# A two-layer block in float32 on one core: the first loads on two queues, two weight products moved ahead of the first transposes, and no subtraction on GpSimd

## The chip, the cores and the metric

The kernel runs on one core of a Trainium2 chip. The metric is the device time of one execution in microseconds; the time of a kernel is the median of several runs. A core has five engines with an instruction queue each: TensorE (PE, matrix products; its weight loads are listed apart as PEld), VectorE (DVE), ScalarE (ACT), GpSimd (POOL) and SyncE (SP, here used only to issue DMA transfers). Each engine takes its instructions in the order that was fixed when the program was built.

## The reference

The input x has 4 sequences of 512 tokens of 256 features. Two layers follow, both of the form x + s * silu(f):

```
xn = layernorm(x)                                    # no scale, no shift
layer 0: s = xn + rmsnorm(((xn W_in^T) * g) W_out^T) * norm_w     # g: one number per channel, from B and C
layer 1: s = xn + causal_attention(layernorm(xn) * gamma + beta) o_proj
both:    f = fwht(silu(xn W1^T) * (xn W3^T)) W2^T    # hidden size 1024, fwht = Walsh-Hadamard transform
x = x + s * silu(f)
```

Everything is float32. The state of the layer 0 mixer is zero at its start and is not carried, so that the mixer is one matrix M = W_in^T diag(g) W_out^T. The transform is symmetric and is applied to W2 in place of the hidden values. In layer 1 the products q k^T and v o_proj need only Wq Wk^T / 16 and Wv o_proj, two products of weights.

## The kernel before, in words

A float32 operand is kept as a pair (hi, lo), hi rounded by ScalarE (a cast, L61) and lo = value - hi by a subtraction (L62), mostly on VectorE; `split` (L59) does both. A float32 product is three products of such parts (`mm3`, L64). Products of weights (`product_of_weights`, L153: wqk, wvo, m) take float32 operands directly.

The work runs sequence by sequence: for b in 0 to 3 the feed-forward block of layer 0 (`ffn`, L310), then the four of layer 1. A feed-forward block has 8 chunks of 128 hidden channels. A chunk c is two up products of 12 matmuls in all into two PSUM banks (f_0gu in the first block, of three banks in the tag), ScalarE's silu of the first bank (L363), VectorE's gate product with the second bank (L364, f_0h), the split of the result (into f_0hh and f_0hl, or into the spare tiles early in the first block), and 12 down products (f_0dn, L332). In the first block all down products come after all up products, since W2 is not ready earlier.

Other work is cut into steps and laid beside the chunks (`Beside`, L530): preparing W2 (`prep_w2`, L113: three butterfly stages of two VectorE operations for each half of the columns, tiles w2b, then a product with the Hadamard matrix into w2ps and a split into w2h and w2l), the mixer, the norm of the next sequence, attention. The build orders the instructions of each engine with a planner: it simulates the program with its own durations and takes, on each engine, the ready instruction that stands earliest in the program. `tc.issue_after(ins)` (L307, L330, L350, L373) pins the instructions of a block behind one instruction of the same engine.

The start (L573 to L629): SyncE issues the four tiles of x for b = 0, then ident, qk, the first part of w13, vo, the second part of w13, w2 (two halves), and the rest (L583 to L594). At the same time TensorE multiplies zeros seven times (L581). `norm_first` (L263) normalises the four token tiles one by one and transposes each (two 128x128 transposes into a PSUM bank, tile xt_0tp), and splits the result into xth and xtl. Then `w13(0)` splits the first part of w13 (`split_w13`, L97, in two halves), and `prep_first` (L607) forms wqk (L608), the three butterfly stages of the first half of w2 and wvo (L615), all ahead of the first block. The parts of w13 that are split later come from `ffn` itself (L351), where each is pinned behind the gate of two chunks before. For parts 2 and 3 the subtraction is on GpSimd (L102); the pin acts on the engines of the gate and so not on GpSimd. The PSUM tag "ms" has three banks, shared by the zero products, the products of weights and the transposes.

Of the kernel before, what the change touches and what calls it, by code (L numbers as in the profile page):

```python
# [12 lines left out]
# float32 kept to the 12 significant bits that one pass of the tensor engine multiplies  # L13
# exactly. A float32 value is the exact sum of two of these (hi + lo), so a float32 product
# is three passes: hi*hi + hi*lo + lo*hi; lo*lo lies below float32's rounding.
# [6 lines left out]
P = 128  # L22
# [6 lines left out]
DS = 16  # L29
# [6 lines left out]
def kernel(ctx: ExitStack, tc: tile.TileContext, a: dict, out: bass.AP):  # L36
# [22 lines left out]
    def split(src, hi, lo, engine=nc.vector):  # L59
        """hi + lo = src, exactly."""  # L60
        nc.scalar.copy(hi, src)  # L61
        engine.tensor_tensor(lo, src, hi.bitcast(F32), ALU.subtract)  # L62

    def mm3(o, terms):  # L64
        """o = sum over terms of lhs.T @ rhs, each operand a pair (hi, lo)."""
        seq = [(l[0], r[0]) for l, r in terms]
        for l, r in terms:
            seq += [(l[0], r[1]), (l[1], r[0])]
        for n, (l, r) in enumerate(seq):
            nc.tensor.matmul(o, l, r, start=n == 0, stop=n == len(seq) - 1)  # L70

# [20 lines left out]
    def load_w13(layer, q):  # L92
        raw = t4(f"w13raw_{layer}_{q}", [P, 2, S])
        nc.sync.dma_start(raw, a[f"w13_{layer}"][q])
        return raw

    def split_w13(layer, q, raw):  # L97
        hi = wp.tile([P, 2, S], F32R, tag="w13h", name=f"w13h_{layer}_{q}", bufs=4)
        lo = wp.tile([P, 2, S], F32R, tag="w13l", name=f"w13l_{layer}_{q}", bufs=4)
        for c in range(2) if (layer, q) == (0, 0) else (slice(None),):  # L100
            cs = slice(c * D, (c + 1) * D) if c in (0, 1) else c
            engine = nc.gpsimd if layer == 0 and q >= 2 else nc.vector  # L102
            split(raw[:, :, cs], hi[:, :, cs], lo[:, :, cs], engine)
        return hi, lo
# [8 lines left out]
    def prep_w2(layer, raws, dst, scratch):  # L113
        """Rows of W2 under the Walsh-Hadamard transform (it is symmetric, so it may act on
        W2 in place of the hidden values): over the 8 blocks by butterflies, over the 128
        rows of a block by a product with the +-1/32 matrix."""
        w2h, w2l = dst
        for half in range(2):
            ds_ = slice(half * P, (half + 1) * P)
            cur = raws[half]  # L120
            for st, h in enumerate((1, 2, 4)):
                nxt = scratch(f"w2b{st}_{layer}_{half}", [P, NH, P])
                cv = cur.rearrange("p (g two h) d -> p g two (h d)", two=2, h=h)
                nv = nxt.rearrange("p (g two h) d -> p g two (h d)", two=2, h=h)
                nc.vector.tensor_tensor(nv[:, :, 0], cv[:, :, 0], cv[:, :, 1], ALU.add)  # L125
                nc.vector.tensor_tensor(nv[:, :, 1], cv[:, :, 0], cv[:, :, 1], ALU.subtract)
                cur = nxt
                yield
            # in float32 it costs TensorE two passes more, but no split beforehand
            native = layer == 0 and half == 0  # L130
            if not native:
                bh = t4(f"w2bh_{layer}_{half}", [P, NH, P], F32R)
                bl = t4(f"w2bl_{layer}_{half}", [P, NH, P], F32R)
                split(cur, bh, bl)
                yield
            for q in range(2):
                o = psum(f"w2ps_{layer}_{half}_{q}", [P, NH // 2, P])
                qs = slice(q * NH // 2, (q + 1) * NH // 2)
                if native:
                    nc.tensor.matmul(o, had_f, cur[:, qs, :], start=True, stop=True)  # L140
                else:
                    nc.tensor.matmul(o, had, bh[:, qs, :], start=True, stop=False)
                    nc.tensor.matmul(o, had, bl[:, qs, :], start=False, stop=True)
                split(o, w2h[:, qs, ds_], w2l[:, qs, ds_])
                yield
# [6 lines left out]

    def product_of_weights(name, lhsT, rhs, nk, scale=None):  # L153
        """[256, 256] = lhsT.T @ rhs over nk chunks of 128, in float32, as a (hi, lo) pair."""
        hi = wp.tile([P, 2, D], F32R, name=f"{name}h")
        lo = wp.tile([P, 2, D], F32R, name=f"{name}l")
        o = psum(f"{name}ps", [P, 2, D])
        for i in range(2):
            for k in range(nk):
                nc.tensor.matmul(  # L160
                    o[:, i, :], lhsT(k, i), rhs(k), start=k == 0, stop=k == nk - 1
                )
        if scale is None:
            split(o, hi, lo)
        else:
            nc.scalar.mul(hi, o, scale)
            nc.vector.scalar_tensor_tensor(lo, o, scale, hi.bitcast(F32), ALU.mult, ALU.subtract)
        return hi, lo
# [9 lines left out]
    def prep_m(win, wout):  # L178
        """xi*(sum of C_real*B_real - C_imag*B_imag) between W_in and W_out is one matrix."""
# [16 lines left out]
    def load_pair(name):  # L196
        raw = t4(f"{name}raw", [P, 2, 2, D])
        nc.sync.dma_start(raw, a[name])
        return raw
# [12 lines left out]
    def moments(name, x, mr):  # L212
        """mr[:, 0] = the tokens' means, mr[:, 1] = their 1 / sqrt(variance + eps)"""
# [10 lines left out]
    def layernorm(name, x, y, groups=(NT,)):  # L224
        """y = layernorm(x), the token tiles in groups of these sizes"""
# [37 lines left out]
    def norm_first():  # L263
        """norm(0, 0), each token tile on its own"""
# [4 lines left out]
        layernorm("ln0_0", xs[0], xn, (1,) * NT)  # L269
        for t in range(NT):  # L270
            o = psum(f"xt0_0tp{t}", [P, 2, P])
            for k in range(2):
                nc.tensor.transpose(o[:, k, :], xn[:, t, sl(k)], ident)
            split(o, hi[:, :, sl(t)], lo[:, :, sl(t)])

    def norm(layer, b):
# [6 lines left out]
        if layer:  # L283
            # The second normalisation acts on the transposed values: its moments as rows of
            # all tokens, in every partition.
# [24 lines left out]
    def ffn(name, xT, w13, w2, slot, defer=1, spare=(), last=None, parts=1, behind=False):  # L310
        """Up, silu gate, down with the transformed W2: two PSUM banks of two token tiles.
        The down products of a chunk follow the up products of the defer-th after it.
        spare: pairs of tiles that hold the split hidden values of the first chunks.
        last: called with each token tile's result, finished one after the other, each in a
        bank of its own."""
# [8 lines left out]
        def down(c, hh, hl, tiles=range(NT)):  # L324
            for t in tiles:
                o = outs[t]
                for n, (l, r) in enumerate(((hh, w2h), (hh, w2l), (hl, w2h))):
# [8 lines left out]
                    # A start clears the accumulate bits of its whole bank: the bank's second  # L336
                    # tile begins without one, behind the first's.
# [44 lines left out]
        # the later tokens' products stay behind, for the ends of the earlier tokens to run beside  # L382
# [11 lines left out]
    def gate(name, dn, s, x, store=None):  # L394
        """x += s * silu(dn), a pair of token tiles at a time."""
# [9 lines left out]
    def mixer(b):  # L405
        """xn += rmsnorm(xn @ M) * norm_w"""
# [21 lines left out]
    def attention(b):  # L428
        """The transposed xn, split; then xn += causal attention of the normalised, scaled and
        shifted xn"""  # L430
# [30 lines left out]
        def scores(i0):  # L461
            """Masked scores of two query tiles"""
# [11 lines left out]
        def softmax(i0, scs):  # L474
            """The two exponentials follow each other, for ScalarE changes its table for them."""
# [54 lines left out]
    class Beside:  # L530
        """Steps of other work, spread over the slots of a feed-forward block."""
# [27 lines left out]
    def some(gen, n):  # L559
        """The next n steps of gen"""  # L560
# [8 lines left out]
    # steps of each; an attention's first ones (up to its scores) run a phase ahead of the rest  # L569
    NORM, MIXER, ATT, ATT1, W2P = 3, 3, 18, 6, 12  # L570

# [1 line left out]
    load_x(0, 1)  # L573
    # TensorE's clock rises only after a while of work: these products of zeros run while the
    # first loads are under way.
# [5 lines left out]
    for i in range(7):  # L581
        nc.tensor.matmul(warm, zr[:, :P], zr, start=True, stop=True)
    nc.sync.dma_start(ident, a["ident"])  # L583
    qk = load_pair("qk")
    raw13 = [load_w13(0, 0)]
    vo = load_pair("vo")
# [8 lines left out]
    norm_first()  # L595
# [7 lines left out]
    w13(0)  # L603
    w2 = w2_tiles(0)
    first = {}

    def prep_first():  # L607
        first["wqk"] = prep_qk(qk)  # L608
        nc.scalar.copy(had, had_f)
        yield  # L610
        steps = prep_w2(0, raw2, w2, x_slot)
        for _ in range(3):
            next(steps)
        yield
        first["wvo"] = prep_vo(vo)  # L615
# [7 lines left out]
    dn = None  # L623
    for b in range(B):
        tasks = []
        if b == 0:
            prep = prep_first()
            for _ in range(3):
                next(prep)  # L629
# [70 lines left out]
def _rows(w):  # L700
    """[r*128, n] -> [128, r, n]"""
# [3 lines left out]
def _w13(w1, w3):  # L705
    """Columns of W1.T and W3.T in turns of 128, in four parts of [128, 2, 512]."""
# [4 lines left out]
def _w2(w2):  # L711
    """W2.T as [half of d][128, 8 blocks, 128]."""
# [46 lines left out]
```

## Time and profile before

The median of 3 runs is 374.34 us (374.17 to 375.75).

| what | before |
|---|---|
| median of the runs | 374.34 us |
| profiled execution, first to last instruction (span) | 370.9 us |
| own time of the profiled execution beside that span | the page gives none; the median of the runs is 3.4 us above the span |
| TensorE busy | 361.5 us, 97% |
| VectorE busy | 248.0 us, 67% |
| ScalarE busy | 179.7 us, 48% |
| GpSimd busy | 36.2 us, 10% |
| DMA moved, 0 to 5 us and 5 to 12 us | 127 and 383 GB/s |
| first up product starts | 9.8 us |

The profile is one execution, recorded by the hardware. Its times start with the first instruction. A row names the line of the kernel, the engine and the tiles (out<-in); "[2.5 <- ...]" or a line of the waits says how long an engine stood idle and whose result ended that. The chain of work is followed back from the last instruction, at each step to what released it. Ends of matmuls are modelled, so a busy TensorE is not one at its peak. A duration of one operation is longer than the distance to the next on the same engine, since neighbours overlap at their ends.

### The profile page before, as it was taken

How to read it: one execution, taken by the hardware profiler on the slowest of the kernel's cores; microseconds unless marked ns; L12 is line 12 of the kernel's file. 1: busy time of each engine (PE TensorE's matmuls, PEld its weight loads, DVE VectorE, ACT ScalarE, POOL GpSimd, SP SyncE). 2: the span in 40 equal slices, each digit the busy share in tenths (PEclk: the TensorE clock that was granted, in tenths of full speed). 3: DMA queues.
4: the chain of work that ended last, by engine and by line, in shares of the span. 5: the costliest groups of instructions: out<-in, count | busy, mean ns of one | idle time of the engine just before them, and what ended most of it. 6: DMA issues, size and time to landing. Idle time of an engine off the chain costs nothing.

```text
span 370.9 us, 5491 instructions
## 1 busy us (share of the span) xinstructions
PE 361.5 (97%) x2167; PEld 318.2 (86%) x2167; DVE 248.0 (67%) x519; ACT 179.7 (48%) x334; POOL 36.2 (10%) x30
## 2 busy tenths in 40 slices
PE   6997999999999999999999999999999999999995
PEld 4875999888888898889888998988989898888895
DVE  6898948996499339945949487465846447374644
ACT  2765334624453335445553654266633646356451
POOL 2060023410025002400011000010000000000000
PEclk9999999999999999999999999999999999999999
DMA  7915200000000040110010001100003000010001
GB/s 234 389 51 203 80 2 1 2 0 2 0 3 0 0 171 0 58 57 2 1 59 0 0 2 57 59 1 2 0 2 114 2 0 1 2 57 2 1 2 57
DMA packets 8969, 15.50 MB, mean 42 GB/s; under 512 B 848, under 2 KB 6640, under 8 KB 8944
## 3 DMA queue, kind: packets, MB, share of 16 engines
q1 hardware_dynamic: 8944, 15.16, 11.7%
q8 instruction: 17, 0.28, 0.3%
q14 instruction: 8, 0.07, 0.1%
HBM read 13.04 MB, written 2.11 MB: 41 GB/s over the span
## 4 chain that ended last, share of the span: by engine, by line
PE 90%; DVE 5%; DMA 2%; SPq 1%; issue 0%; ACT 0%; DVEq 0%
PE f_3gu L70 12%; PE f_2gu L70 12%; PE f_1gu L70 12%; PE f_0gu L70 8%; PE f_0dn L332 6%; PE f_3dn L332 6%; PE f_1dn L332 6%; PE f_2dn L332 6%; PE sc L70 4%; PE pv L70 4%; PE o L70 3%; PE v L70 3%; PE tq L70 3%; DMA w2raw<-in_w 2%; DVE w2b L125 1%; PE pt L498 1%
## 5 line engine op out<-in xcount | busy, mean ns | idle before, releaser
L70 PE MATMUL f_0gu<-xtl,w13h 128*128 128x512 f32 (+1 forms) x68 | 25.8, 382 | 0.0
L70 PE MATMUL f_1gu<-xth,w13l 128*128 128x512 f32 x64 | 25.5, 399 | 0.0
L70 PE MATMUL f_0gu<-xth,w13l 128*128 128x512 f32 (+1 forms) x68 | 25.5, 384 | 0.0
L70 PE MATMUL f_3gu<-xtl,w13h 128*128 128x512 f32 x64 | 25.5, 398 | 0.0
L70 PE MATMUL f_2gu<-xth,w13l 128*128 128x512 f32 x64 | 25.3, 396 | 0.0
L70 PE MATMUL f_3gu<-xth,w13l 128*128 128x512 f32 x64 | 25.3, 396 | 0.0
L70 PE MATMUL f_1gu<-xtl,w13h 128*128 128x512 f32 x64 | 25.3, 396 | 0.0
L70 PE MATMUL f_2gu<-xtl,w13h 128*128 128x512 f32 x64 | 25.3, 395 | 0.0
L70 PE MATMUL f_0gu<-xth,w13h 128*128 128x512 f32 (+1 forms) x68 | 21.3, 393 | 2.5 <-DVE f_0h L364 2.5
L364 DVE TENSOR_TENSOR f_2h<-f_2h,f_2gu 128x512 f32<-128x512 f32 x16 | 10.9, 681 | 19.1 <-PE f_2gu L70 11.0
L61 ACT CAST f_2hh<-f_2h 128x512 fp32r<-128x512 f32 x16 | 9.9, 621 | 23.0 <-DVE f_2h L364 23.0
L70 PE MATMUL f_2gu<-xth,w13h 128*128 128x512 f32 x64 | 20.7, 397 | 0.0
L70 PE MATMUL f_1gu<-xth,w13h 128*128 128x512 f32 x64 | 20.7, 398 | 0.0
L70 PE MATMUL f_3gu<-xth,w13h 128*128 128x512 f32 x64 | 20.6, 397 | 0.0
L61 ACT CAST f_3hh<-f_3h 128x512 fp32r<-128x512 f32 x16 | 9.9, 620 | 19.7 <-DVE f_3h L364 19.7
L332 PE MATMUL f_3dn<-w2l,f_3hh 128*128 128x256 f32 x64 | 17.6, 281 | 0.0
L332 PE MATMUL f_2dn<-w2l,f_2hh 128*128 128x256 f32 x64 | 17.6, 282 | 0.0
L332 PE MATMUL f_3dn<-w2h,f_3hh 128*128 128x256 f32 x64 | 17.5, 281 | 0.0
L332 PE MATMUL f_2dn<-w2h,f_2hh 128*128 128x256 f32 x64 | 17.5, 281 | 0.0
L332 PE MATMUL f_1dn<-w2l,f_1hh 128*128 128x256 f32 x64 | 17.4, 281 | 0.0
L332 PE MATMUL f_1dn<-w2h,f_1hh 128*128 128x256 f32 x64 | 17.3, 281 | 0.0
L363 ACT ACTIVATE f_2h<-f_2gu 128x512 f32<-128x512 f32 x16 | 9.5, 596 | 16.0 <-PE f_2gu L70 16.0
(227 smaller groups left out, 1104.4 us busy)
## 6 DMA issues: line engine op xcount, KB each, us to landing
w13raw<-in_w SPq DMA_DIRECT2D x8, 512.0 KB, 6.2
w2raw<-in_w SPq DMA_DIRECT2D x4, 512.0 KB, 6.8
mrb<-there SPq DMA_DIRECT2D x4, 512.0 KB, 3.7
x<-in_x SPq DMA_DIRECT2D x3, 512.0 KB, 3.7
out<-x SPq DMA_DIRECT2D x6, 256.0 KB, 2.1
x<-in_x SPq DMA_DIRECT2D x4, 128.0 KB, 2.2
qkraw<-in_qk SPq DMA_DIRECT2D x1, 512.0 KB, 4.7
voraw<-in_vo SPq DMA_DIRECT2D x1, 512.0 KB
```

The costliest lines, as they stand in the source:

```text
L61: nc.scalar.copy(hi, src)
L70: nc.tensor.matmul(o, l, r, start=n == 0, stop=n == len(seq) - 1)
L125: nc.vector.tensor_tensor(nv[:, :, 0], cv[:, :, 0], cv[:, :, 1], ALU.add)
L332: return nc.tensor.matmul(o, l[:, sl(t)], r[:, c, :], start=start, stop=stop, skip_group_check=True)
L363: nc.scalar.activation(h, gu[0], AF.Silu)
L364: gates.append(nc.vector.tensor_tensor(h, h, gu[1], ALU.mult))
L498: nc.tensor.transpose(pt[:, sl(j)], p[:, sl(j)], ident)
```

## The change

ident, qk and vo are issued by ScalarE, directly behind the issue of x by SyncE; the first part of w13 follows on SyncE. The zero products are five instead of seven. The product wqk is formed ahead of the first transposes, which are pinned behind its last matmul; wvo is formed between the transposes of tiles 1 and 2, pinned in the same way. The split of the first w13 part is pinned behind the splits of tile 1, and the first butterflies of w2 behind the last low part of tile 3. The subtraction of every w13 part is on VectorE. `last_product` remembers the last matmul of each product of weights.

```diff
-    def load_w13(layer, q):
+    def load_w13(layer, q, queue=nc.sync):
         raw = t4(f"w13raw_{layer}_{q}", [P, 2, S])
-        nc.sync.dma_start(raw, a[f"w13_{layer}"][q])
+        queue.dma_start(raw, a[f"w13_{layer}"][q])
...
-            engine = nc.gpsimd if layer == 0 and q >= 2 else nc.vector
-            split(raw[:, :, cs], hi[:, :, cs], lo[:, :, cs], engine)
+            split(raw[:, :, cs], hi[:, :, cs], lo[:, :, cs])
...
+    last_product = {}
...
-                nc.tensor.matmul(
+                last_product[name] = nc.tensor.matmul(
...
     def load_pair(name):
         raw = t4(f"{name}raw", [P, 2, 2, D])
-        nc.sync.dma_start(raw, a[name])
+        nc.scalar.dma_start(raw, a[name])
...
+        behind, lo_ = last_product["wqk"], None
         for t in range(NT):
+            if t == 2:
+                with after(behind):
+                    first["wvo"] = prep_vo(vo)
+                behind = last_product["wvo"]
             o = psum(f"xt0_0tp{t}", [P, 2, P])
-            for k in range(2):
-                nc.tensor.transpose(o[:, k, :], xn[:, t, sl(k)], ident)
-            split(o, hi[:, :, sl(t)], lo[:, :, sl(t)])
+            with after(behind):
+                for k in range(2):
+                    behind = nc.tensor.transpose(o[:, k, :], xn[:, t, sl(k)], ident)
+            hi_ = nc.scalar.copy(hi[:, :, sl(t)], o)
+            lo_ = nc.vector.tensor_tensor(
+                lo[:, :, sl(t)], o, hi[:, :, sl(t)].bitcast(F32), ALU.subtract
+            )
+            if t == 1:
+                with after(hi_), after(lo_):
+                    w13(0)
+        return lo_
...
     load_x(0, 1)
+    nc.scalar.dma_start(ident, a["ident"])
+    qk = load_pair("qk")
+    vo = load_pair("vo")
+    raw13 = [load_w13(0, 0)]
...
-    for i in range(7):
+    for i in range(5):
         nc.tensor.matmul(warm, zr[:, :P], zr, start=True, stop=True)
-    nc.sync.dma_start(ident, a["ident"])
-    qk = load_pair("qk")
-    raw13 = [load_w13(0, 0)]
-    vo = load_pair("vo")
     raw13 += [load_w13(0, 1)]
...
-    norm_first()
+    first = {"wqk": prep_qk(qk)}
...
-    w13(0)
+    normed = norm_first()
     w2 = w2_tiles(0)
-    first = {}
 
     def prep_first():
-        first["wqk"] = prep_qk(qk)
         nc.scalar.copy(had, had_f)
-        yield
         steps = prep_w2(0, raw2, w2, x_slot)
-        for _ in range(3):
-            next(steps)
-        yield
-        first["wvo"] = prep_vo(vo)
+        with after(normed):
+            for _ in range(3):
+                next(steps)
         yield
...
             prep = prep_first()
-            for _ in range(3):
-                next(prep)
+            next(prep)
```

## The prediction

> **What bounds the kernel now.** I read four views: the busy times of the page, the waits of TensorE, the chain of work cut to the first 45 us, and the order of time of VectorE and GpSimd in the stretch where TensorE stands still. First the busy times (us, share of the span, instructions), then who TensorE waited for over the whole span (us in total, times, longest).
>
> ```profile
> PE 361.5 (97%) x2167; PEld 318.2 (86%) x2167; DVE 248.0 (67%) x519; ACT 179.7 (48%) x334; POOL 36.2 (10%) x30
> ```
>
> ```profile
> PE f_0gu L70 <- DVE f_0h L364: 2.5, 1, 2.5
> PE warm L582 <- DVE zr L579: 1.9, 1, 1.9
> PE xt_0tp L273 <- DVE ln_0r L237: 0.5, 1, 0.5
> PE xt_0tp L273 <- DVE xtl L62: 0.3, 1, 0.3
> PE xt_0tp L273 <- DVE xn L240: 0.2, 1, 0.2
> ```
>
> TensorE is the bound: from 31.4 us to its last product it waits for nothing. So an edit can gain only in what stands in front: one stall of 2.5 us, three small ones before the first transposes (1.0 us together), and a start at 5.8 us, ahead of which there are only products of zeros. Everything later can only get worse. The chain shows who sets the end of the 2.5 us stall (start, us, what):
>
> ```profile
> 4.96 7.99 DMA w2raw<-in_w
> 12.97 0.69 DVE w2b L125
> ...
> 15.59 0.60 DVE wvol L62
> 16.19 0.59 DVE f_0h L364
> 16.79 1.14 DVE w13l L62
> ...
> 22.13 2.24 DVE early L62
> 24.36 2.81 DVE w2b L125
> ...
> 30.17 0.60 DVE w2b L126
> 30.77 0.61 DVE f_0h L364
> 31.38 0.04 issue
> 31.43 1.66 PE f_0gu L70 x6
> ```
>
> From the landing of the first w2raw at 12.95 to 31.4 us VectorE works without a pause, and TensorE waits for the gate product (L364) at its end, which frees a PSUM bank of the up products. Two links of that chain are about four times too long. Beside them lies GpSimd (start, us, engine, line, shape, count):
>
> ```profile
> 20.31 6.31 POOL L62 TENSOR_TENSOR w13l<-w13raw,w13h 128x1024 fp32r<-128x1024 f32 x2 [13.46 <-ACT w13h L61]
> ...
> 22.04 2.32 DVE L62 TENSOR_TENSOR early<-f_0h,early 128x512 fp32r<-128x512 f32 x1
> 24.29 2.88 DVE L125 TENSOR_TENSOR w2b<-w2b 128x512 f32<-128x512 f32 x1
> 27.09 0.68 DVE L126 TENSOR_TENSOR w2b<-w2b 128x512 f32<-128x512 f32 x1
> ```
>
> The same two operations take 0.68 us each elsewhere (median of the w2b rows 0.68, of the early rows 0.68) and follow each other 0.60 apart. The two long ones both read two SBUF tiles while GpSimd reads two. They start at 22.04 and 24.29, the next at 27.09: (2.25 - 0.60) + (2.80 - 0.60) = 3.85 us lost.
>
> **The change, part by part.**
>
> No split on GpSimd: the two low-part subtractions of w13 parts 2 and 3 (3.50 and 2.87 us on GpSimd) become VectorE's. Price: the row of part 1, 128x1024 at 1.22 us, 1.14 to the next instruction; two of them 2.28 us. VectorE wins back the 3.85. Net -1.57 us of VectorE time.
>
> Both now carry a wait: the part 2 split stands behind chunk 2's gate on VectorE, part 3 behind chunk 4's. Behind them queue the butterflies, low parts and gates of the later chunks, and TensorE waits for those through its PSUM banks. Whether one or both fall ahead of chunk 3's gate (the one that ended the stall) isn't visible, so I keep +1.14 and +2.28.
>
> Product of vo ahead: its eight products take 1.73 us (0.216 apart) whichever place they have, so TensorE's work is unchanged; but wvol (0.60 us in the chain at 15.59) leaves the chain.
>
> Start of the chain: the w2 butterflies now wait for the last low part of the first transposes, tile 3. I put that at 11.6 us below, when w2raw has landed too (12.95 before; the loads come earlier, see below). Against 12.97: -1.3.
>
> The gate at the end of the chain, at 31.4, so moves by -3.85 - 0.60 - 1.3 + (1.14 to 2.28) = -4.6 to -3.5, to 26.8 to 27.9 us. TensorE arrives at 28.9 (28.4 with the start below). The 2.5 us stall goes with 0.5 to 1.6 us to spare. That margin is the cover of the added 2.28; gone, each further us on VectorE is a us of TensorE. Next late would be part 3's low part: chunk 4 ends on TensorE at about 26.9, gate and split follow by 28.6, chunk 6 wants it at about 30. ScalarE loses nothing: its casts for these parts stay.
>
> Two queues. SyncE issues one load per 0.47 us, so qk went out as the sixth. With the page's DMA rates by stage (us, PE, PEld, DVE, ACT, POOL busy, clock, DMA share, GB/s):
>
> ```profile
> 0.00:5.00 5.00, 3.09 (x7) 2.15 (x7) 2.81 (x10) 1.28 (x1) 0.58 (x6) 1.00 0.59 127
> 5.00:12.00 7.00, 5.96 (x32) 4.48 (x32) 5.21 (x17) 3.29 (x8) 1.84 (x4) 1.00 0.96 383
> ```
>
> The first 5 us move 127 GB/s, the next seven 383. ScalarE can issue ident, qk, vo from 0.73 (three issues at 0.43 beside its table load of 1.28 us, 2.6 us in all before its first cast, which came at 6.5). Here a rule speaks against the edit: the Trainium skill, "DMA: Bandwidth & Descriptors", section "Issuing engines are not separate DMA queues", says that all issuers share the same 16 engines and a second one saves only issue time. By it nothing is won once they are full; by the row they are not full for the first 5 us. qk was issued at 3.06 and landed 4.7 us later, 7.8. Issued at 1.2, with the x tiles beside it, x + ident + qk are 1.1 MB: at 383 GB/s from 2.4 us on, 5.3. Both ends: 4.3 (qk preferred) and 7.8 (no gain). I take 5.2. vo now precedes the first w13 part (2.2 MB in all): 2.4 + 2.2/0.383 = 8.1, against 9.1 before. If the second queue wins nothing it is 9.1 + 1.3 = 10.4. SyncE's own queue loses three issues, so w13 and w2raw go out 1.4 us sooner. The price falls on x: its four tiles landed by 4.6 and now share the engines, to 5.3 by the same sum, 7 if the big packets of qk and vo are preferred. Tile 0 needed 2.9 us from its landing to its normalised value, the later ones some 2, and their transposes stand behind the two products (7.4 and 10.2 below), which hides it.
>
> TensorE's start. Transposes are ordered behind the qk product, tiles 2 and 3 behind vo's. Five zero products instead of seven end near 4.1. A second rule is against it: "TensorE: Matmul & The Clock Gate", Part 1, grants the full clock only after some 3.4 us of sustained work. The row: the zero products' weight loads took 330 ns, those of the transposes 143 (median; up to 229, at 5.8 us), and no stage shows a granted clock other than 1.00, so the rise can be placed only at about 6.3. If it stays there, the qk product runs 5.2 to 7.4 (2.5 of its eight at half speed). If the gap before qk costs one more window, half of 3.4 us, 1.7, is lost: the end would be 371.3 + 1.7 = 373.0. I take the first, as the qk product itself fills the stretch.
>
> Then: transposes of two tiles 0.6 (8.0); vo's product needs one of three PSUM buffers, free when the qk result is copied (0.60 ScalarE, 0.68 VectorE): 0.5 of waiting (8.5); product 1.7 (10.2); two tiles 0.6 (10.8), low part of tile 3 by 11.6. The up products start at about 10.9, under w13's cast. Before, TensorE had both products and all transposes behind it at 12.93, with 13 half-width up products (0.117 apart, 1.5 us) mixed in: 11.4. Gain 0.5; with the ends of qk's landing -1.5 to +1.4.
>
> Sum: -2.5 (stall) - 0.5 (start) = -3.0 on a span of 370.9, 367.9. The profile gives no other time of its own; the runs' median is 374.34, 3.4 above the span. With that unchanged: **371.3 us**.
>
> **The rivals.** A measurement of this kernel can tell about 0.5% from no change: 372.5 to 376.2 is "the same".
>
> *The start eats the gain.* The stall goes, but the clock rises a window later (-1.7), or qk lands near 7.8, pinning the transposes behind it (up to 2.0 worse than my value). 371.3 + 1.7 = 373.0. For it: DMA share is 0.96 from 5 us on, and all loads share it; TensorE idles about 1 us before qk. Against: the first 5 us are half empty. The form in which the edit doesn't do what it says (the second queue moves nothing) is the milder end: gain 0 in place of 0.5, 371.8.
>
> *VectorE becomes the bound of the first block: slower.* In 11 to 41 us it is busy 27.3 of 30. If the order written out by the planner puts the part 2 split behind all butterflies (twelve at 0.60, the low parts and gates of three chunks), it comes at 11.6 + 7.2 + 1.2 + 1.1 + 1.8 + 1.8 + 1.1 = 25.8, where TensorE wants it at about 24: 1.8 of stall at chunk 4; with gate 4 late by as much, part 3 behind the mixer's and the next norm's work (4.2 us of statistics at 39.5) stalls chunk 6 by up to 4. Total 5.8 against 2.5 before, less 0.5: 377.1. It decides once the two splits come over 4.9 us late together. Against: without GpSimd VectorE has 1.57 us less to do.
>
> **How the numbers follow.** Stall gone: 0.60, own range 370.0 to 372.4 (qk landing early to the second queue useless, and a stall of half a us left). Gain eaten: 0.24, about 373, to 375. Slower: 0.16, about 377. So faster 0.60, same 0.24, slower 0.16. The range leaves out some 0.05 below 370.0 and most of the slower case above 376.3.
>
> **What would show it.** No GpSimd row at L62; early and w2b rows all near 0.68; no wait of TensorE for f_0h near 28; qk landing by 5.5 and the first 5 us above 200 GB/s; qk product from about 5.2, with weight loads falling from 330 to 190 ns within it; up products from about 11; nothing new after 41 us. I am wrong if TensorE waits for w13l in chunks 4 or 6, if the qk product starts near 7.8, or if weight loads stay at 330 ns past 7 us.

## The result, and the profile after

The changed kernel takes 374.38 us (median of 20 runs), the kernel before 373.91 (20 runs, taken beside it). The ratio is 1.001, with a 95% interval of 0.999 to 1.003: no difference that can be measured. The forecast was 371.3 us, faster. Seven of the 20 executions take 372.2 to 373.1 us at a mean granted clock of 0.997 to 1.000, thirteen take 374.1 to 376.6 us, ten of these at 0.989 to 0.995.

The profiled execution has a span of 370.4 us, against 370.9; it took 372.17 us, the least of the 20. Each execution takes 1.8 to 2.0 us more than its span, so of the 3.4 us that the forecast added to the span only about 1.8 lie outside it. The rest means that the profile of the kernel before, too, shows an execution shorter than the median (by estimate 370.9 + 1.8 = 372.7 us). First the waits of TensorE after the change (us in total, times, longest):

```profile
PE warm L602 <- DVE zr L599: 1.9, 1, 1.9
PE wvops L161 <- DVE wqkl L168: 1.5, 1, 1.5
PE wqkps L161 <- DMA qkraw<-in_qk: 0.8, 1, 0.8
PE f_0dn L347 <- ACT w2h L61: 0.4, 1, 0.4
```

The stall of 2.5 us on the gate product is gone. In its place stands a wait of the vo product for the low part of the qk product, 1.5 us, with two smaller ones (the 1.9 us are the start of the program, as before). The long VectorE rows are gone too (order of time, VectorE, the same stretch as before):

```profile
22.17 0.68 DVE L62 TENSOR_TENSOR early<-f_0h,early 128x512 fp32r<-128x512 f32 x1
22.77 0.68 DVE L379 TENSOR_TENSOR f_0h<-f_0h,f_0gu 128x512 f32<-128x512 f32 x1
23.37 1.22 DVE L62 TENSOR_TENSOR w13l<-w13raw,w13h 128x1024 fp32r<-128x1024 f32 x1
24.50 0.68 DVE L124 TENSOR_TENSOR w2b<-w2b 128x512 f32<-128x512 f32 x1
...
28.10 0.68 DVE L379 TENSOR_TENSOR f_0h<-f_0h,f_0gu 128x512 f32<-128x512 f32 x1
...
30.70 1.22 DVE L62 TENSOR_TENSOR w13l<-w13raw,w13h 128x1024 fp32r<-128x1024 f32 x1
```

Every early and w2b operation is at 0.68 us, the two added low parts (w13l) take 1.22 each as the forecast priced them, and TensorE waits for neither. What went wrong lies before all this. The chain of work of the changed kernel, cut to the start (start, us, what):

```profile
2.10 6.29 DMA x<-in_x
...
8.41 0.44 DVE ln_0st L234
...
9.33 0.56 POOL ln_0r L239
...
9.91 0.28 DVE xn L241
...
10.24 0.70 DVE wqkl L168
...
10.98 1.99 PE wvops L161 x8
12.97 0.48 PE f_0gu L70 x4
```

The last tile of x (tile 3, counted from 0) landed at 8.4 us; before the change it had landed by 4.6. VectorE does that tile's norm, which includes a step on GpSimd, and then the low part of the qk product (wqkl), whose inputs had been ready since 9.6. This low part is the last reader of the qk product's PSUM bank, and of the three shared banks it is the one that the vo product gets; so the vo product waits for it. The up products start at 12.6 us where the forecast had 10.9, and where the kernel before started at 9.8 with part of its products still to do. The DMA rates by stage, and the rows of the qk product:

```profile
0.00:5.00 5.00, 2.50 (x5) 1.49 (x5) 2.40 (x8) 1.28 (x1) 0.86 (x6) 1.00 0.64 201
5.00:12.00 7.00, 5.29 (x17) 4.12 (x18) 4.61 (x15) 3.01 (x6) 1.66 (x3) 1.00 0.99 387
```

```profile
L161 PEld LDWEIGHTS wqkps<-qkraw x8: 288/337/337, 5.2 to 7.9; 128*128 128x128 f32 x8
L161 PE MATMUL wqkps<-qkraw x8: 634/634/796, 5.2 to 8.3; 128*128 128x256 f32 x8
```

The second queue did fill the first 5 us (201 GB/s, before 127), and qk landed at 5.13. But the qk product ran at half speed to its end: its eight matmuls took 3.6 us (5.17 to 8.75), where the vo product's took 1.6 (10.98 to 12.62), and its weight loads 337 ns where the vo product's took 190. The clock column stands at 1.00 in both stages, so this slow start shows in the durations alone.

### The profile page after: what moved, and what is told of

Same layout as the page of the kernel before. It is cut to its first block, busy times and chain, and to the rows that moved or that the text cites. A ratio compares the mean times of both kernels' runs of the same rounds, so it can differ in the third digit from the quotient of the medians.

```text
span 370.4 us, 5483 instructions
## 1 busy us (share of the span) xinstructions
PE 361.8 (98%) x2165; PEld 318.9 (86%) x2165; DVE 244.8 (66%) x521; ACT 179.7 (49%) x334; POOL 33.1 (9%) x28
## 3 DMA queue, kind: packets, MB, share of 16 engines
q1 hardware_dynamic: 8512, 14.05, 10.9%
## 4 chain that ended last, share of the span: by engine, by line
PE 96%; DMA 2%; DVE 1%; SPq 0%; ACT 0%; issue 0%; POOL 0%
PE f_0gu L70 12%; PE f_3gu L70 12%; PE f_2gu L70 12%; PE f_1gu L70 12%; PE f_0dn L347 6%; PE f_3dn L347 6%; PE f_1dn L347 6%; PE f_2dn L347 6%; PE sc L70 4%; PE pv L70 4%; PE o L70 3%; PE v L70 3%; PE tq L70 3%; DMA x<-in_x 2%; PE pt L513 1%; PE mps L161 1%
## 5 line engine op out<-in xcount | busy, mean ns | idle before, releaser
L70 PE MATMUL f_0gu<-xth,w13l 128*128 128x512 f32 (+1 forms) x68 | 25.2, 381 | 0.0
L379 DVE TENSOR_TENSOR f_2h<-f_2h,f_2gu 128x512 f32<-128x512 f32 x16 | 10.9, 684 | 18.2 <-PE f_2gu L70 10.1
```

The costliest lines, as they stand in the source:

```text
L379: gates.append(nc.vector.tensor_tensor(h, h, gu[1], ALU.mult))
```

## The experiments

Two theories stood against each other. One: the change is two parts that cancel, a stall removed and a start made later. The other: the stall was worth nothing, because VectorE's next late result takes its place.

**GpSimd part alone**, on the kernel before:

```diff
-            engine = nc.gpsimd if layer == 0 and q >= 2 else nc.vector
+            engine = nc.vector
```

> The kernel before with one edit: the low parts of w13 parts 2 and 3 on VectorE, the start as it was. If the change is two parts that cancel (the stall of 2.5 us goes, the start gives it back), this is about 2.3 us faster than before: 371.6, ratio 0.994, no wait of TensorE at 28.9, and the early and w2b rows all near 0.68 us. If the stall was worth nothing because the next late thing on VectorE takes its place, the ratio is 1.000 and a new wait of TensorE between 24 and 40 us shows it.

372.03 us, ratio 0.9953 (0.9932 to 0.9974): faster by 1.0 to 2.5 us. The waits of TensorE:

```profile
PE xt_0tp L273 <- DMA ident<-in_ident: 1.0, 1, 1.0
PE f_0dn L332 <- ACT w2h L61: 0.5, 1, 0.5
```

The stall is gone and was worth something; VectorE's early and w2b rows in 20 to 32 us are all at 0.68 us. The middle of the interval is 1.75 us, not 2.5; a new wait of 0.5 us for w2h, at 35 us, is part of the difference (the changed kernel has it too).

**The new start alone**: the changed kernel with GpSimd's subtractions back.

```diff
-            split(raw[:, :, cs], hi[:, :, cs], lo[:, :, cs])
+            engine = nc.gpsimd if layer == 0 and q >= 2 else nc.vector
+            split(raw[:, :, cs], hi[:, :, cs], lo[:, :, cs], engine)
```

> The changed kernel with one part undone: the low parts of w13 parts 2 and 3 on GpSimd again, the new start kept. If the two parts cancel, this shows the new start alone with the old stall: about 2.2 us slower than before, 376.1, ratio 1.006, two VectorE rows of 2 to 3 us at 20 to 28 us. If the start costs nothing and the stall gave nothing, the ratio is 1.000.

376.88 us, ratio 1.0087 (1.0053 to 1.0122). The start costs 2 to 4.5 us when the old stall stays. Two VectorE rows of 2.31 and 2.87 us are back at 22.9 and 25.2 us. TensorE waits 2.0 us for the low part of the qk product and 1.6 for gate products, and after the first of these waits, which begins at 9.7, the granted clock falls (the column before the last two):

```profile
10.00:12.00 2.00, 0.30 (x1) 0.30 (x2) 1.36 (x4) 2.00 (x4) 0.55 (x1) 1.00 1.01 400
12.00:14.00 2.00, 2.00 (x9) 1.69 (x7) 1.51 (x3) 0.28 (x1) 0.00 (x0) 0.72 1.08 359
14.00:16.00 2.00, 2.00 (x10) 1.91 (x10) 0.69 (x1) 0.89 (x2) 0.00 (x0) 0.50 1.10 374
```

The theory that the stall was worth nothing falls with this pair: one part gains, the other loses. Their middles add up to about +1.5 us, the two together measured +0.4; the intervals are wide enough for both.

**The clock.** Seven products of zeros again:

```diff
-    for i in range(5):
+    for i in range(7):
```

> The changed kernel with seven products of zeros again in place of five. They end at about 5.1 us, when qk lands (5.13), so they cover the 1.4 us in which TensorE stood still. If the late rise of the clock (qk product with weight loads of 330 ns to 8.7 us) is one of the two costs of the start, the rise comes earlier in most executions, the qk product ends up to 1.7 us sooner and the median falls by about 1 us, 373.4. If the clock is not the cause, 374.4 as the changed kernel.

374.05 us, ratio 1.0009 (0.9991 to 1.0027): nothing won, although in this profile the qk product ended at 7.8 in place of 8.7. The reason is in the waits and in the chain of this kernel:

```profile
PE wvops L161 <- DVE wqkl L168: 3.3, 1, 3.3
```

```profile
1.65 5.64 DMA x<-in_x
...
8.81 0.41 DVE xn L241
9.22 0.34 DVE ln_0st L234
...
10.62 0.04 DVE xn L241
...
10.95 0.69 DVE wqkl L168
```

An earlier end of the qk product only lengthens the wait behind it. Two norms of late tiles, each with a round trip to GpSimd, stand on VectorE ahead of the low part. In this profile the wait, and not the late rise of the clock, sets the start of the vo product.

**The bank.** The vo product in a bank of the tag of the up products, which is empty at that time:

```diff
-        o = psum(f"{name}ps", [P, 2, D])
+        o = psum(f"{name}ps", [P, 2, D], **bank)
...
-            "wvo", lambda k, i: vo[:, 0, k, sl(i)], lambda k: vo[:, 1, k, :], 2
+            "wvo", lambda k, i: vo[:, 0, k, sl(i)], lambda k: vo[:, 1, k, :], 2, None, {"tag": "gu", "bufs": 3}
```

> The changed kernel with the vo product in a PSUM bank of the up products (unused then) in place of one of the three shared ones. If the wait of 1.5 us of the vo product on the qk product's low part is the other cost of the start, the vo product starts right behind the first transposes (about 9.4 in place of 11.0), the up products at about 11.3 in place of 12.6, and the median falls by about 1.2 us, 373.2. If the first up products then wait for w13's casts and low parts instead, less than 0.4 is won.

371.67 us, ratio 0.9960 (0.9944 to 0.9976). The wait is gone from the list and the up products start at 11.5:

```profile
PE warm L602 <- DVE zr L599: 1.9, 1, 1.9
PE wqkps L161 <- DMA qkraw<-in_qk: 0.7, 1, 0.7
PE f_0dn L347 <- ACT w2h L61: 0.4, 1, 0.4
```

That is 2.7 us below the changed kernel's median (374.38), taken in another series of runs. By the ratios to the kernel before (1.001 and 0.996, each measured in its own series) it is 1.9 us, more than the 1.2 expected. All twelve executions lie between 371.1 and 372.2 us at a granted clock of 0.997 or more: about 1 us below the seven shorter ones of the changed kernel, and the thirteen longer ones have no counterpart.

**The cause of the late low part.** Three kernels ask whether it is the late x, the order on VectorE, or the second queue. First, vo behind x on SyncE's queue:

```diff
-    vo = load_pair("vo")
+    vo = load_pair("vo", nc.sync)
```

> The changed kernel with one transfer moved: vo is issued by SyncE behind the four tiles of x in place of by ScalarE behind qk. If the late x (tile 3 at 8.4 us) is what holds VectorE, and with it the qk product's low part and the vo product, then tile 3 lands by about 6.3, the qk low part follows the qk product at about 9.6 in place of 10.2 to 11.0, TensorE waits at most 0.8 us for it in place of 1.5 to 3.3, and the median falls by about 1.5 us, 372.9. If the wait has another cause, 374.4.

371.87 us, ratio 0.9965 (0.9950 to 0.9980): 2.5 us below the changed kernel by the medians and 1.7 by the ratios, with one transfer moved. In the profile, which is of an execution of 373.7 us, the vo product ran at half speed, too, from 10.6 to 13.8. Tile 3 of x lands at 6.2, and the wait is 0.6:

```profile
PE wqkps L161 <- DMA qkraw<-in_qk: 1.0, 1, 1.0
PE wvops L161 <- DVE wqkl L168: 0.6, 1, 0.6
```

Second, the queues alone, on the kernel before:

```diff
-        nc.sync.dma_start(raw, a[name])
+        nc.scalar.dma_start(raw, a[name])
...
-    nc.sync.dma_start(ident, a["ident"])
+    nc.scalar.dma_start(ident, a["ident"])
```

> The kernel before with the queues alone: ident, qk and vo issued by ScalarE; the products, transposes and GpSimd as before. If the second queue is what makes x late, tile 3 lands past 7 us in place of 4.6, and as the transposes come first here they wait for it: 0 to 1.5 us slower than before, ratio 1.000 to 1.004. If an earlier issue simply wins, the up products start before 9.8 us and it is 0.5 us faster, ratio 0.9985.

375.27 us, ratio 1.0052 (1.0032 to 1.0073): slower, a little beyond what was expected. Tile 3 lands at 8.0 and the transposes wait for the norms. During the longer wait the granted clock falls as well, to 0.50 from 8.4 to 15.0 us, and the qk product runs at half speed, so the loss in this profile is the wait and the slower clock behind it:

```profile
PE xt_0tp L273 <- DVE xn L240: 3.4, 2, 2.7
```

Third, the order on VectorE: the norms of tiles 2 and 3 pinned behind the low part of qk, loads and banks as in the changed kernel.

```diff
+            if n == 1 and i >= 2:
+                stack.enter_context(after(low_part["wqk"]))
```

> The changed kernel with one order on VectorE turned round: the norms of token tiles 2 and 3 stand behind the qk product's low part in place of ahead of it; the banks and the loads are as in the changed kernel. If the wait came from that order (the low part queued behind a norm that waits for a late x), the vo product starts at about 10.2 or earlier, right behind the low part, and the median falls by about 1 us, 373.4, although tiles 2 and 3 are now transposed later. If the bank itself was the trouble, the vo product waits on and it stays at 374.4.

373.76 us, ratio 1.0023 (1.0010 to 1.0035): no gain shown. The median is 0.6 us below the changed kernel's, but the ratio to the kernel before is not lower (1.0023, the changed kernel's 1.001); 1 us was expected. The vo product starts at 10.6 and waits 0.6 us, as after moving vo; but tiles 2 and 3 are now transposed late (14.4 to 15.1), with waits of 0.5 us for their norm and 0.5 for their copy. So in the profile the order on VectorE made the length of the wait, and turning it round passes the late x on to the next thing.

**The clock once more**, now with the bank repaired (the edits of the third and fourth kernel together).

> The changed kernel with both: the vo product in a bank of its own and seven products of zeros. The bank alone gave 371.7, seven zero products alone nothing (374.0). If the seven gave nothing only because the vo product waited for the low part whatever the clock did, they show now: the clock rises earlier in part of the executions and the median falls by 0.5 to 1 us below 371.7. If the two missing zero products cost nothing in any case, 371.7.

371.64 us, ratio 0.9962 (0.9949 to 0.9974), the same as the bank alone. The profile is of an execution of 373.2 us; the 22 take 371.2 to 373.3. In it the vo product ends at 9.9, and then the transposes of tile 2 wait 1.9 us for the same low part, which holds a shared bank. In this execution the gain was again swallowed. Its stages (us, then busy PE, PEld, DVE, ACT, POOL, granted clock, DMA share, GB/s) show that the granted clock falls behind this wait, too:

```profile
10.00:12.00 2.00, 0.06 (x1) 0.00 (x0) 1.30 (x5) 1.87 (x4) 0.55 (x1) 1.00 1.01 397
12.00:14.00 2.00, 2.00 (x13) 1.91 (x14) 2.00 (x5) 1.38 (x5) 0.00 (x0) 0.80 1.09 351
14.00:16.00 2.00, 2.00 (x11) 1.90 (x10) 2.00 (x5) 1.19 (x1) 0.00 (x0) 0.50 1.10 364
```

**Both repairs**, vo on SyncE and a bank of its own:

> The changed kernel with both repairs: vo issued by SyncE behind x, and the vo product in a bank of the up products. Alone they gave 371.9 and 371.7. If both take away the same wait (of the vo product for the low part), together they give no more: 371.6. If each takes away a part of its own, about 371.0.

371.56 us, ratio 0.9945 (0.9924 to 0.9966): no clear gain over either alone. That fits one wait, which both take away.

**Both repairs with eight products of zeros**, which end when qk lands:

> As the kernel with both repairs, with eight products of zeros, which end when qk lands (5.4). No wait is left between them and the up products that could swallow an earlier rise of the clock. If the half clock of the qk and vo products costs time, up to 0.9 us is won in executions in which the clock rises by 7 us: 371.2 or below. If not, as without.

370.40 us, ratio 0.9919 (0.9899 to 0.9938): 3.0 us faster than the kernel before and the fastest of all. Its six executions lie within 0.3 us (370.37 to 370.66), all below the six of the kernel with both repairs (370.86 to 371.79). TensorE waits for nothing but the first zeros and w2h:

```profile
PE warm L602 <- DVE zr L599: 1.9, 1, 1.9
PE f_0dn L347 <- ACT w2h L61: 0.4, 1, 0.4
```

```profile
5.50 3.02 PE L161 MATMUL wqkps<-qkraw 128*128 128x256 f32 x8
8.36 0.60 PE L280 MATMUL xt_0tp<-ident,xn 128*128 128x128 f32 x4
8.79 1.89 PE L161 MATMUL wvops<-voraw 128*128 128x256 f32 x8
10.54 0.44 PE L280 MATMUL xt_0tp<-ident,xn 128*128 128x128 f32 x2
10.73 0.72 PE L70 MATMUL f_0gu<-xth,w13h 128*128 128x256 f32 x4
```

The up products start at 10.7, for the forecast's 10.9, but not by its sum: the qk product lasts until 8.1 for its 7.4, and the 0.5 us of waiting don't come. With the wait gone, the three further zero products are worth 1.2 us (371.56 to 370.40). The clock rises earlier in the profile: the weight loads of the vo product take 190 ns (median; at most 192), against 305 (at most 337) without the three.

**A second queue for the small load only**: the kernel before, low parts on VectorE, ident alone on ScalarE.

> The kernel before with the low parts on VectorE (372.0) and ident alone issued by ScalarE; x, qk, w13, vo stay on one queue in the old order. If the second queue helps where it carries only what is small, the first transposes no longer wait 1.0 us for ident and it falls by 0.3 to 1 us, 371.0 to 371.7, at or below the best of the changed kernel's repairs. If the start hides ident anyway, 372.0.

372.94 us, ratio 0.9976 (0.9957 to 0.9995), no better than the low parts alone (372.03). The wait for ident is gone, but the transposes wait 1.4 us for their norms, and the planner wrote another order, with a new wait of 1.2 us of the up products for a silu. What of this is the load and what the order stays open.

## Why the prediction was wrong, step by step

The removal of the stall was right in its mechanism: GpSimd's subtraction stretched VectorE's operations beside it, the stretch moved the gate, the gate held TensorE. (That the shared reads of SBUF are the reason was not tried apart from that.) Its size was forecast at 2.5 us; alone it is 1.75 (1.0 to 2.5). The low parts' price (1.22), their places (23.4 and 30.7) and the absence of a wait for them were right. VectorE was not the bound: that rival did not happen, though the butterflies began at 14.9 and not at 11.6.

The start was forecast as a gain of 0.5 us. In the profile TensorE has both products and all transposes behind it at 13.7, less 0.5 for the four up products mixed in: 13.2 against 11.4 before, a loss of 1.8. With the 0.4 for w2h and the 2.5 of the stall, the sum is -0.3; the spans differ by -0.5. Against the forecast the start is 2.3 us late, and two terms make up about that: 1.0 us more waiting for the PSUM bank, and 1.4 us more for the qk product.

*"Price falls on x ... which hides it."* This is the step that failed. The forecast put tile 3 at 5.3, at worst 7; it landed at 8.4. Its sum counts x, ident and qk and leaves out vo. But ScalarE issued vo at 1.65 us, ahead of tile 3 at 2.10, and vo landed first, at 8.2; with vo moved behind x, tile 3 landed at 6.2. By the forecast's own rate, x, ident, qk and vo (1.64 MB) would have ended at 6.7, an estimate. The rates by stage give 2.3 MB moved by 8.4 us, an estimate, too, so that loads issued later (w13 from 2.58 us on) shared the engines with them. And the delay isn't hidden: the forecast asked only when the transposes would want tile 3, and not what is queued behind its norm on VectorE. The low part of qk is, and behind that the PSUM bank of vo. The "0.5 of waiting" for that bank was 1.5 us in the profile, 3.3 in that of the kernel with seven zero products; shortening it in two different ways gave 1.9 and 1.7 us by the ratios. That this is more than 1.0 fits the thirteen longer executions: ten of them have a lower granted clock, and the kernel with GpSimd's subtractions, which has the same start, shows the clock falling to 0.50 behind this wait. No profile shows a longer execution of the changed kernel itself.

*The clock.* The forecast kept its rise at 6.3 us, so that 2.5 of the eight qk matmuls would be slow. All eight were: 3.6 us in place of 2.2. The rule of the Trainium skill, "TensorE: Matmul & The Clock Gate", Part 1, that the full clock comes only after some 3.4 us of sustained work, agrees with this profile: the qk product starts at 5.17 us, behind a pause, and the weight loads are short from 8.75. The forecast weighed it as a rival at 373.0, with 1.7 us by estimate; the term measured 1.4. But an earlier rise alone won nothing, as the seven zero products show; its 1.2 us appeared only when no wait behind it could swallow them.

The rival "the start eats the gain" is what came, by one of its two named routes and a third. The clock rose later, as named; qk did not land late; the longer wait for the bank it did not name. The Trainium skill, "DMA: Bandwidth & Descriptors", section "Issuing engines are not separate DMA queues", says that a second issuer saves only issue time and that all transfers interleave on the same engines. Here the saved issue time did bring qk sooner (5.1 us for 7.8), and the interleaving was paid by x. The forecast named this price and sized it too small.

## What to carry to other kernels

When a load moves to a second queue, ask which loads of the first queue are issued after it and now land later, and follow the delayed one through its consumer's queue: behind an in-order wait there can stand something that a third engine needs. A removed stall and a lengthened start of similar size leave no trace in the time; two kernels, each with one part, show it. And a repair upstream of a wait (here the clock) can measure as nothing until the wait is gone.

## What the runs showed that was not expected

The granted clock can fall again after a short pause of TensorE. In the kernel with the bank and seven zero products TensorE pauses for about 2 us from 9.9, and the granted clock is 0.50 from 13.2 to 16.6; in the changed kernel with GpSimd's subtractions the pause is as long, from 9.7, and the clock is 0.50 from 12.9 to 16.3. So such a wait can cost twice, once as idle time and once as slower work after it. It need not: in the changed kernel with seven zero products a pause of 3.3 us left the granted clock at 1.00. What decides is not shown.

The loads of the two queues landed in the order of their issue, whichever queue they were on: in the profile of the changed kernel qk (issued at 1.17 us) landed at 5.1, x's third tile (1.64) at 6.0, vo (1.65) at 8.2 and x's fourth tile (2.10) at 8.4. So the second queue put vo ahead of the x tile that the first had not yet issued. Whether the size of the transfers sets the shares was not tried.
